# The scan's first loads, clears and diagonal pieces as operations of the stages' plan, in one lasting tile

## The chip, the cores and the metric

The kernel runs on one NeuronCore of a Trainium2 chip. The metric is device time in microseconds, the median of several executions of the same program; lower is better. The profile is one further execution.

## The reference

Eight images of 96 channels and 64 × 64 pixels go through a state-space block with a residual, then through linear attention and a quantized feed-forward, each with a residual. What matters here, cut down:

```python
xi, z = split(layernorm(gn(x)) @ in_proj_w.T + in_proj_b)   # 192 channels each
xi = silu(depthwise_conv3x3(xi) + conv_b)
xs = stack([rows(xi), columns(xi)]); xs = concat([xs, flip(xs)])  # 4 directions, L = 4096
dts, Bs, Cs = split(einsum("bkdl,kcd->bkcl", xs, x_proj_w))       # 6, 16, 16
delta = softplus(dt_proj(dts) + dt_proj_b)
for t in range(L):                                          # 192 channels x 16 states
    h = exp(delta[t] * A) * h + (delta[t] * u[t]) * B[t]
    y[t] = (h * C[t]).sum(states)
out = (layernorm(sum_of_directions(y + D * u)) * silu(z)) @ out_proj_w.T + out_proj_b
```

## The kernel before

The images go in four pairs. For each pair there is a stage and then a scan; a fifth stage finishes the last pair. Between them nothing overlaps but what the queues let through.

**A stage** holds up to five streams of work. For the new pair: `project` (norms, input projection, gate; 16 chunks of 512 positions), `convolve` (3 × 3 depthwise; two channel groups on VectorE in steps at L537 and L540, one on TensorE), `prepare` (states B and C, step sizes delta, delta × u, for 4 directions and 8 chunks in three channel groups, VectorE at L670 to L686; the results `dl`, `du`, `bs`, `cs` go to DRAM). For the old pair: `back` (reads the scan's output `ys` into `yk`, adds directions at L984, norm, gate, output projection, key-value product; 16 units) and `tail` (attention and feed-forward, last add on GpSimd at L1134, store; 16 units). The first stage has no old pair, the last no new one. In the first stage the weights are laid out too, among them the scan's decay matrices `awd`.

**The order in a stage** is made by a planner (`Plan`). Each operation has an engine, an estimated cost, the names that it reads and writes, and a rank. On each engine, among operations that could start within 0.1 us of the earliest by the estimates, that of the lowest rank is put next; so ranks share out an engine, and what is ready fills gaps. The six numbers `FRONT`, `CONV`, `PREP`, `BACK`, `TAIL`, `TAIL_END` set the ranks: project runs from 0 to `FRONT`, convolve from there to `CONV`, prepare from `PREP` to 1, back from 0 to `BACK`, tail from `TAIL` to `TAIL_END`. `P.also` names a gate that every operation added while it is set reads; `gate_off` adds an operation that waits until all of these are done. All DMAs are issued by SP, in the plan's order. A `Slab` cuts one SBUF tile into parts by hand.

**The scan** has an order written out by hand: for 128 steps of 128 positions (4 directions × 32), eight pieces each. A piece is six decay matmuls (`aw` × `dm`, L837), an Exp on ScalarE (L842, L844) and a recurrence on VectorE (L855, 774 columns). GpSimd makes the driving term `dbu` from `dut` and `bc` for two pieces at a time (L819). TensorE then sums the states with a diagonal of C, `cw`: eight of its sixteen column groups are ScalarE copies of `bc` with a mask (L773), eight are small loads (L779), and the rest of those eight is zero from the start (clears at L715, L716). `aw` and `dm` are loaded at L730, L745 and L746, `bc` at L757, `dut` at L792. All these tiles belong to pools that are opened for the scan, in memory that the stage's pools held before; SP issues aw, dm, dut and bc when the stage's last users have let go of it.

Of the kernel before, what the change touches and what calls it, by code (L numbers as in the profile page):

```python
# [19 lines left out]
DIM = 96  # L20
DI = 192
NS = 16
# [16 lines left out]
FRONT = 0.05  # L39
CONV = 0.35  # L40
PREP = 0.08
BACK = 0.7
TAIL = 0.66
TAIL_END = 1.29
NE = 24
X0 = F - 3 * SEG
WC = 256
LOGEXP = "natural_log_exp_and_others"
# [9 lines left out]
class Plan:  # L58
# [9 lines left out]
    def __init__(self):  # L68
        self.ops, self.wrote, self.read = [], {}, {}
        self.free, self.left, self.tiles, self.home = {}, {}, {}, {}  # L70
        self.unit = self.also = None
        self.claims = set()
# [7 lines left out]
    def add(self, engine, cost, emit, reads=(), writes=(), new=(), rank=0.0, kind=None, size=0.0):  # L80
        i = len(self.ops)
        after = set()
        if self.also:
            reads = (*reads, self.also)
# [86 lines left out]
def vss_attn_ffn(ctx: ExitStack, tc: tile.TileContext, a: dict):  # L171
# [96 lines left out]
    class Slab:  # L268


        def __init__(self, pool, name, size):
            self.all, self.at = pool.tile([128, size], F32, name=name), 0
# [46 lines left out]
    def weights(P, wp):  # L319

        P.also = "A3"
# [38 lines left out]
        P.also = None  # L360

    def decay_weights(P, wp):
# [28 lines left out]
        for k in range(KD):  # L391
# [10 lines left out]
            dma(P, 1.6, lambda k=k: awd[k], lambda w=w: P[w].rearrange("p c m n -> p (c m n)"), (w,), (),  # L402
# [16 lines left out]
    def project(P, pair, zs, ybuf, p1, beside):  # L419
# [17 lines left out]
        for b in range(2):  # L437
            mv, gm, gd, gv, gr = stat[b]
            X, S = f"xt{pair}.{b}", f"stat{b}"
            P.also = f"A1.{b}"  # L440
# [67 lines left out]
        P.also = None  # L508
# [4 lines left out]
    def convolve(P, xi, ybuf, p1, beside):  # L513

        P.also = "A2"
# [52 lines left out]
        P.also = None  # L568
# [18 lines left out]
    def prepare(P, tmp, xi, us, dl, du, bs, cs_, beside):  # L587
        P.also = "A2" if beside else "A3"
# [22 lines left out]
        dlv = dl.rearrange("k c a m e t -> k c a (m e) t")  # L611
        duv = du.rearrange("k c m e t -> k c (m e) t")
        for o in range(2):
            for c in range(NCH):
# [14 lines left out]
                for k in (o, o + 2):  # L629
# [17 lines left out]
                    for v, r in ((bs, RK), (cs_, 32 + RK)):  # L647
                        for b in range(2):
                            dma(P, 0.035, lambda v=v, k=k, c=c, b=b: v[
                                    k, 2 * c : 2 * c + 2, NS * b : NS * b + NS].rearrange("j p t -> p j t"),  # L650
                                lambda S=S, r=r, b=b: P[S][64 * b + r : 64 * b + r + NS].rearrange(
                                    "p (j t) -> p j t", j=2), (S,), (), (), rank)
# [12 lines left out]
                    for T in range(3):  # L665
# [7 lines left out]
                        spread(P, 0.26, lambda o, n, k=k, j=j: duv[k, j, o : o + n].rearrange("j p t -> p j t"),  # L673
                               T, lambda q=q: P[q].rearrange("p (j t) -> p j t", t=TC), (q,), (), rank)
# [4 lines left out]
                        def high(name):  # L679
# [11 lines left out]
                        spread(P, 0.39, lambda o, n, k=k, c=c: dlv[  # L691
                                   k, c * F // WC : (c + 1) * F // WC, :, o : o + n
                               ].rearrange("j a p t -> p (j a) t"),
                               T, lambda dp=dp: P[dp].rearrange("p j a t -> p (j a) t"),
                               (dp + "#0", dp + "#1", dp + "#2"), (), rank)


    def scan(dl, du, bs, cs_, ys):
        with ExitStack() as st:
# [6 lines left out]
            quad = st.enter_context(tc.tile_pool(name="s4", bufs=5))  # L706
# [5 lines left out]
            cw = [one.tile([128, 2, NB, 16, TC], F32, name=f"cw{i}") for i in range(2)]  # L712
            for t in da + yp:
                nc.vector.memset(t, 0.0)
            nc.vector.memset(cw[0], 0.0)  # L715
            nc.gpsimd.memset(cw[1], 0.0)  # L716
            da = [t[:, X0 : X0 + W6 + 1] for t in da]

# [5 lines left out]
            aw, dm, bc, dut, dbu, hs, yev = {}, {}, {}, {}, {}, {}, {}  # L724

            def load_aw(k, r):

                aw[k, r] = one.tile([128, NI, 2, 128], BF16, name=f"aw{r}")
                w = 2 * NI * 128
                nc.sync.dma_start(  # L730
                    aw[k, r].rearrange("p i z m -> p (i z m)"), awd[k, :, r * w : r * w + w]
                )

            def load(s, part):
# [4 lines left out]
                if s % 2 == 0 and part == 0:  # L739
                    dm[s // 2] = wk.tile([128, NE, WC], BF16, name="dm")  # L740
                w = NE // 4
                o = 2 * w * (s % 2) + w * part
                v = dl[k, c // 2, :, :, o : o + w].rearrange("a m e t -> (a m) (e t)")
                to = dm[s // 2][:, o : o + w].rearrange("p e t -> p (e t)")
                nc.sync.dma_start(to[0:96], v.unsqueeze(1).to_broadcast([48, 2, w * WC]))  # L745
                nc.sync.dma_start(to[96:128], v[0:32])  # L746

            def load_bc(s):
# [4 lines left out]
                i = s // NB  # L753
                bc[i] = wk.tile([128, 2, 2, NB * TC], F32, name="bc")
                for w, v in ((1, cs_), (0, bs)):
                    for b in range(2):
                        nc.sync.dma_start(  # L757
                            bc[i][64 * b : 64 * b + 64, w].rearrange("p z t -> p (z t)"),
                            v[k, c // NB, 16 * b : 16 * b + 16]
                            .rearrange("(n z) t -> n (z t)", z=2)  # L760
                            .unsqueeze(0).to_broadcast([8, 8, 2 * NB * TC]),
                        )
                        yield

            def diagonal(s):
# [5 lines left out]
                i = s // NB  # L771
                for m in range(8):
                    nc.scalar.activation(  # L773
                        cw[i % 2][:, :, :, m, :].rearrange("p z j t -> p (z j) t"),
                        bc[i][:, 1].rearrange("p z (j t) -> p (z j) t", j=NB),
                        AF.Copy, scale=blk[:, m : m + 1],
                    )
                    m += 8
                    nc.sync.dma_start(  # L779
                        cw[i % 2][8 * m : 8 * m + 8, :, :, m, :].rearrange("p z j t -> p (z j) t"),  # L780
                        cs_[k, c // NB, 16:32].rearrange("(n z) (j t) -> n (z j) t", z=2, j=NB),
                    )
                    yield

            def fetch(g):

                if g >= 4 * N:
                    return
                k, c, _ = steps[g // 4]
                o = NI * (g % 4)  # L790
                dut[g] = quad.tile([128, NI, TC], F32, name="dut")
                nc.sync.dma_start(  # L792
                    dut[g].rearrange("p i t -> p (i t)"),
                    du[k, c, :, o : o + NI].rearrange("m i t -> m (i t)").unsqueeze(1)
                    .to_broadcast([16, 8, NI * TC]),
                )
# [4 lines left out]
            def drive(g):  # L801
# [13 lines left out]
                else:  # L815
# [5 lines left out]
                    dut[g].unsqueeze(1)  # L821
                    .to_broadcast([128, 2, NI, TC]),
                    bc[s // NB][:, 0, :, bass.ts(c % NB, TC)].unsqueeze(2)
# [4 lines left out]
            def decay(p):  # L828
# [7 lines left out]
                for i in range(NI):  # L836
                    nc.tensor.matmul(  # L837
                        e[:, i], aw[k, r][:, i, z, :], dm[s // 2][:, NI * r + i, bass.ts(c % 2, TC)],
# [54 lines left out]
            for r in range(NR):  # L893
                load_aw(0, r)
            for j in range(2):
                load(0, j)
            fetch(0)
            for _ in load_bc(0):
                pass
            fetch(1)  # L900
            for j in range(2):
                load(1, j)
            for _ in diagonal(0):
                pass
            fetch(2)
# [31 lines left out]
    def back(P, pair, ys, us, zs, t1, tn, tmp, psm, kept=None):  # L937
        if kept is None:
            tns = ring(P, tmp, "tns", 3, [DIM + 1, F])
# [8 lines left out]
        yks = ring(P, tmp, "yk", 2, [128, KD, 8, 4 * NE])  # L948
        yds = ring(P, tmp, "yd", 2, [128, 2, 4, 8 * NE])
# [366 lines left out]
```

## Time and profile before

| | us |
|---|---|
| median of 3 runs (10145.36 to 10156.27) | 10145.48 |
| the profiled execution, its own time | 10155.55 |
| its span, first to last instruction | 10153.8 |
| stage 0, to the first recurrence at 529.1 | 529.1 |
| scans (529.1–2310.1, 3028.0–4810.4, 5529.7–7310.5, 8030.1–9807.9) | 1781.0, 1782.4, 1780.8, 1777.8 |
| middle stages between them | 717.9, 719.3, 719.6 |
| last stage | 345.9 |
| busy: VectorE, GpSimd, TensorE, ScalarE | 9133.4, 7542.1, 7238.0, 7028.9 |

A row of the timeline begins with the start and the busy time of a run of like instructions, then engine, line, operation and tiles (out <- in), and in brackets how long the engine was idle before and what ended that. `SPq` is SP issuing a DMA. In the stages many tiles are parts of slabs, so their rows bear the slab's name (`A`), and helpers give one line to many operations (L296 activations, L315 DMAs).

### The profile page before, as it was taken

The numbers are of one execution on the slowest core, as the hardware profiler recorded it, in microseconds if no ns is written. First come the engines' busy times: TensorE is split into PE (matmuls) and PEld (weight loads), VectorE is DVE, ScalarE is ACT, GpSimd is POOL, SyncE is SP. The second block draws the span as 40 slices with busy tenths as digits, with TensorE's granted clock in tenths as the row PEclk, the third lists the DMA queues.
The fourth block names the chain that finished last, engine by engine and source line by source line (L and its number), as shares of the span: only waits on it lengthen the run. The fifth ranks groups of instructions, "written<-read, shape, count | busy, mean of one in ns | idle before, by whom it ended". The sixth has DMA issues, their size and how long they took to land. (4 is left out here: it accounts for less than half of the span.)

```text
span 10153.8 us, 382989 instructions
## 1 busy us (share of the span) xinstructions
PE 7238.0 (71%) x166080; PEld 5184.5 (51%) x166080; DVE 9133.4 (90%) x7072; ACT 7028.9 (69%) x12289; POOL 7542.1 (74%) x2416
## 2 busy tenths in 40 slices
PE   6666676667876667666886666666688666676678
PEld 2155565554425556555442555555543355565554
DVE  7699999997679999999778999999877899999985
ACT  5667777776777777776677777777667777777754
POOL 2099999991039999999104999999810599999971
PEclk7689989998878998988887999998888799988989
DMA  4988888886988888887698888878769788788884
GB/s 132 235 211 215 214 215 213 214 213 138 241 216 213 214 214 216 213 214 188 165 243 211 211 215 213 217 212 214 191 167 240 208 213 216 212 216 214 213 193 102
DMA packets 1593915, 2085.10 MB, mean 205 GB/s; under 512 B 409891, under 2 KB 1050404, under 8 KB 1588644
## 3 DMA queue, kind: packets, MB, share of 16 engines
q1 hardware_dynamic: 1592228, 2060.59, 78.3%
q8 instruction: 1304, 21.36, 1.0%
q14 instruction: 383, 3.14, 0.1%
HBM read 1601.99 MB, written 458.04 MB: 203 GB/s over the span
## 5 line engine op out<-in xcount | busy, mean ns | idle before, releaser
L855 DVE TENSOR_TENSOR_SCAN h<-da,dbu 128x774 f32<-128x774 f32 x4096 | 7025.9, 1759 | 139.5 <-POOL dbu L819 43.5
L819 POOL TENSOR_TENSOR dbu<-dut,bc 128x1536 f32<-128x1536 f32 x2048 | 7083.4, 3575 | 73.6 <-DMA dm<-dl 30.2
L844 ACT ACTIVATE da<-da 128x768 f32<-128x768 f32 x4092 | 3260.2, 797 | 1984.4 <-PE da L837 1968.0
L837 PE MATMUL da<-dm,aw 128*128 128x128 bf16 x24576 | 2279.9, 235 | 2268.3 <-DVE h L855 2078.8
L837 PEld LDWEIGHTS <-aw 128*128 128x128 bf16 x24576 | 1792.8, 104 | 2512.4 <-issue 2233.3
L873 PE MATMUL yp<-h,cw 128*32 128x48 f32 x131072 | 2904.7, 238 | 101.7 <-issue 88.3
L873 PEld LDWEIGHTS yp<-h,cw 128*32 128x32 f32 x131072 | 2412.1, 154 | 548.4 <-issue 228.3
L773 ACT ACTIVATE cw<-bc,blk 128x512 f32<-128x512 f32 x2048 | 1472.4, 720 | 74.3 <-DMA dut<-du 36.0
L984 POOL TENSOR_TENSOR yd<-yk 128x768 f32<-128x768 f32 x64 | 126.7, 1981 | 918.3 <-DMA yk<-ys 630.4
L1134 POOL TENSOR_TENSOR yk<-yk,yd 96x512 f32<-96x512 f32 x64 | 100.1, 1565 | 775.7 <-issue 406.0
L624 POOL COPY A<-A 128x512 f32<-128x512 f32 x96 | 135.7, 1423 | 676.6 <-ACT A L296 375.2
L881 ACT ACTIVATE yev<-yp 128x384 f32<-128x384 f32 x1024 | 505.4, 494 | 81.6 <-PE yp L873 81.3
L296 ACT ACTIVATE A<-A 128x512 bf16<-128x512 bf16 (+1 forms) x777 | 445.8, 618 | 145.1 <-DMA dl<-A 108.6
L816 ACT COPY dbu<-h 128x12 f32<-128x12 f32 x1984 | 409.2, 206 | 0.0
L682 DVE TENSOR_TENSOR A<-A 128x512 f32<-128x512 f32 x384 | 287.2, 751 | 88.6 <-ACT A L296 87.2
L657 PE MATMUL q<-A 6*64 6x512 f32 x1536 | 301.0, 734 | 78.7 <-ACT A L296 65.5
L686 DVE TENSOR_TENSOR A<-A 128x512 bf16<-128x512 f32 x384 | 279.8, 729 | 83.8 <-DMA dl<-A 81.6
L540 DVE SCALAR_TENSOR_TENSOR A<-A,c_convw,A 128x2048 f32<-128x2048 f32 x128 | 299.2, 2363 | 0.6
L998 PEld LDWEIGHTS q<-ident,yd 128*96 128x96 f32 x2048 | 248.1, 169 | 82.9 <-issue 62.2
L998 PE MATMUL q<-ident,yd 128*96 128x128 f32 x2048 | 260.9, 281 | 15.4 <-DVE yd L984 9.3
L296 ACT ACTIVATE A<-q,c_dtb 128x512 f32<-128x512 f32 x384 | 253.7, 677 | 7.0 <-PE q L657 6.0
L411 PE MATMUL q<-small,c_j 96*96 96x512 f32 x384 | 230.1, 693 | 28.8 <-ACT small L296 19.1
(125 smaller groups left out, 5271.8 us busy)
## 6 DMA issues: line engine op xcount, KB each, us to landing
dut<-du SPq DMA_DIRECT2D x2048, 384.0 KB
dm<-dl SPq DMA_DIRECT2D x1024, 288.0 KB
dl<-A SPq DMA_DIRECT2D x256, 384.0 KB
dm<-dl SPq DMA_DIRECT2D x1024, 96.0 KB
ys<-yev SPq DMA_DIRECT2D x1024, 96.0 KB
du<-A SPq DMA_DIRECT2D x256, 256.0 KB
bc<-cs SPq DMA_DIRECT2D x512, 128.0 KB
bc<-bs SPq DMA_DIRECT2D x512, 128.0 KB
```

The costliest lines, as they stand in the source:

```text
L296: "ACT", cost, lambda: nc.scalar.activation(dst(), src_(), func, **kw),
L540: dve(P, 2.34, lambda o=o, v=v, w=w: nc.vector.scalar_tensor_tensor(o, v, w, o, ALU.mult, ALU.add), (), wr, (), first + (CONV - FRONT) / 2 ...
L657: nc.tensor.matmul(P[pqs[T]][o : o + 64], dtw[at : at + RK, k, o : o + 64], P[S][at : at + RK], start=True, stop=True,)
L773: nc.scalar.activation(cw[i % 2][:, :, :, m, :].rearrange("p z j t -> p (z j) t"), bc[i][:, 1].rearrange("p z (j t) -> p (z j) t", j=NB), ...
L816: nc.scalar.copy(start, segs(hs[s - 1][:, :, r])[:, :, :, 1 if back else TC])
L819: nc.gpsimd.tensor_tensor(segs(t)[:, :, :, 1:], dut[g].unsqueeze(1) .to_broadcast([128, 2, NI, TC]), bc[s // NB][:, 0, :, bass.ts(c % NB, ...
L837: nc.tensor.matmul(e[:, i], aw[k, r][:, i, z, :], dm[s // 2][:, NI * r + i, bass.ts(c % 2, TC)], start=True, stop=True,)
L844: nc.scalar.activation(e, e, AF.Exp)
L855: nc.vector.tensor_tensor_scan(hs[s][:, w, r][:, d], da[p % 3][:, o : o + W6][:, d], dbu[4 * s + r][:, w][:, d], 0.0, ALU.mult, ALU.add,)
L873: nc.tensor.matmul(y[32 * q : 32 * q + 32, 2 * NE * i : 2 * NE * i + 2 * NE] .rearrange("p (j r i) -> p i j r", j=2, r=NR), w[:, z, :, t], ...
L881: nc.scalar.activation(yev[s][:, :, o : o + 8, :].rearrange("p j i e -> p i j e"), y[:, 0 : 16 * NE].rearrange("p (i j e) -> p i j e", j=2 ...
L998: nc.tensor.matmul(o, P[yd][:, k, j, DIM * g : DIM * g + DIM], ident, start=(k + j == 0), stop=(k + j == 4),)
```

## The change

One tile `left` now lasts over the whole program. The scan keeps in it `aw`, two `dm`, two `bc`, three of five `dut` and one `cw`; the stages cut their own tiles from the same memory: back's and tail's `yk`, `yd` and one `tns` lie in the part `LT` (under aw, dm and dut 0), back's other tiles and convolve's diagonal in the rest (under bc, dut 1, dut 2 and cw), in the first stage prepare's and the weights' slab from the start of LT into LB, and `small` under cw. Three gates, LT, LB and LC, tell when each part is free. A new function `begin` adds the scan's first loads, one clear and the first eight diagonal pieces to the plan, at rank 2, behind everything else that is ready; the scan no longer issues them. The other `cw` is cleared by half, on VectorE at the scan's start, and of `da` only the boundary columns are. `dl`, `du`, `bs`, `cs` become one DRAM tensor for each direction. The six rank numbers change. Cut to its core:

```diff
-FRONT = 0.05
-CONV = 0.35
-PREP = 0.08
-BACK = 0.7
-TAIL = 0.66
-TAIL_END = 1.29
+FRONT = 0.35
+CONV = 0.54
+PREP = 0.62
+BACK = 0.6
+TAIL = 0.49
+TAIL_END = 1.5
+LT = 4 * 768 + 2 * 3072 + 768
+LB = 2 * 1024 + 2 * 768
...
@@ convolve
-        P.also = "A2"
+        P.also = ("A2", "LB", "LC") if beside else ("A2",)
@@ prepare
-        P.also = "A2" if beside else "A3"
+        P.also = ("A2",) if beside else ("A3", "LB", "LT")
@@ back
+        P.also = ("LB", "LC", "LT")
@@ tail
+        P.also = ("LT",)
...
+    def begin(P, left, dl, du, bs, cs_):
+
+        two, one = Slab(left[:, 0:LT]), Slab(left[:, LT:])
...
+        for name in ("LB", "LC", "LT"):
+            gate_off(P, name)
+        late = 2.0
+        P.add("POOL", 3.5, lambda: nc.gpsimd.memset(cw[:, :, :, 8:16], 0.0), ("LC",), ("cw",), (), late)
+        for at, (to, v) in enumerate(wide_bc(bc[0], bs, cs_, 0, 0)):
+            dma(P, 0.13, lambda to=to: to, lambda v=v: v, ("LB", "bs.0"), (f"bc#{at}",), (), late)
+        for g in (1, 2, 0):
+            to, v = wide_du(dut[g], du, 0, 0, g)
+            dma(P, 0.4, lambda to=to: to, lambda v=v: v, ("LB" if g else "LT", "du.0"), (), (), late)
+        for r in range(NR):
+            to, v = wide_aw(aw, 0, r)
+            dma(P, 0.4, lambda to=to: to, lambda v=v: v, ("LT", "awd0"), (), (), late)
+        for part in range(4):
+            for to, v in wide_dm(dm[0], dl, 0, 0, part):
+                dma(P, 0.2, lambda to=to: to, lambda v=v: v, ("LT", "dl.0"), (), (), late)
+        for m in range(8):
+            (to, v), (to2, v2) = one_block(cw, bc[0], cs_, 0, 0, m)
+            act(P, lambda to=to: to, lambda v=v: v, AF.Copy, 0.72, ("LC", "bc#0", "bc#1", "w_blk"), (f"cw#{m}",), (),
+                late, scale=blk[:, m : m + 1])
+            dma(P, 0.02, lambda to2=to2: to2, lambda v2=v2: v2, ("cw", "bs.0"), (f"cw#{m + 8}",), (), late)
+        return aw, dm, bc, dut, cw
...
-            for t in da + yp:
-                nc.vector.memset(t, 0.0)
-            nc.vector.memset(cw[0], 0.0)
-            nc.gpsimd.memset(cw[1], 0.0)
+            for t in da:
+                nc.vector.memset(t[:, 0 : W6 + 1 : SEG], 0.0)
+            nc.vector.memset(cw[1][:, :, :, 8:16], 0.0)
...
-            for r in range(NR):
-                load_aw(0, r)
-            for j in range(2):
-                load(0, j)
-            fetch(0)
-            for _ in load_bc(0):
-                pass
-            fetch(1)
-            for j in range(2):
-                load(1, j)
-            for _ in diagonal(0):
-                pass
-            fetch(2)
             fetch(3)
             fetch(4)
```

## The prediction

> **What bounds the kernel now.** I read the page first, then busy time by stretch, then the timeline around the hand-over from a stage to the scan, then the waits there.
>
> ```profile
> DVE  7699999997679999999778999999877899999985
> POOL 2099999991039999999104999999810599999971
> ```
>
> These rows of the page's 40 slices show four scans in which VectorE and GpSimd are both full, and five stages between them in which neither is. Inside a scan nothing is to be had: 1756 of 1781 us are VectorE work. The stages and the joints remain. The first middle stage, cut into stretches (columns: stretch, length, busy us of PE, PEld, DVE, ACT and POOL, clock, DMA share, GB/s):
>
> ```profile
> 2327.00:2480.00 153.00, 128.29 (x417) 62.74 (x418) 110.94 (x135) 102.63 (x156) 13.75 (x7) 0.90 0.77 172
> 2480.00:2560.00 80.00, 65.54 (x762) 35.68 (x763) 58.07 (x44) 59.34 (x86) 10.76 (x7) 0.93 0.47 122
> 2560.00:2730.00 170.00, 154.65 (x722) 79.50 (x722) 113.56 (x165) 108.79 (x173) 15.77 (x9) 0.90 0.98 251
> 2730.00:2992.00 262.00, 216.15 (x698) 60.67 (x699) 213.29 (x365) 213.69 (x368) 47.86 (x31) 0.78 0.85 229
> 2992.00:3008.00 16.00, 6.68 (x20) 1.89 (x18) 10.26 (x22) 7.55 (x14) 4.16 (x5) 0.86 0.25 69
> 3008.00:3022.00 14.00, 2.11 (x18) 1.89 (x19) 7.61 (x3) 0.00 (x0) 6.92 (x2) 0.50 0.95 257
> ```
>
> Until 2560 us TensorE is the fullest (84 and 82%) and DMA has room; from 2560 DMA (251, then 229 GB/s) and three engines are all near full. The last two rows are the joint: first DMA idles while the tail's last chains run out, then the engines idle while the scan's first loads run at 257 GB/s. The joint in order of time:
>
> ```profile
> 3004.56 1.15 POOL L1134 TENSOR_TENSOR yk<-yk,yd 96x512 f32<-96x512 f32 x1 [3.44 <-issue]
> ...
> 3007.88 1.78 SPq L730 DMA_DIRECT2D aw<-awd  x4
> ...
> 3010.48 6.88 DVE L715 MEMSET cw<- 128x8192 f32 x1 [1.70 <-issue]
> ...
> 3016.62 2.11 PE L837 MATMUL da<-dm,aw 128*128 128x128 bf16 x18 [13.26 <-DMA dm<-dl]
> ...
> 3022.19 5.00 ACT L773 ACTIVATE cw<-bc,blk 128x512 f32<-128x512 f32 x8 [18.14 <-DMA dm<-dl]
> 3024.27 3.43 POOL L819 TENSOR_TENSOR dbu<-dut,bc 128x1536 f32<-128x1536 f32 x1 [9.35 <-DMA dm<-dl]
> 3027.10 0.79 ACT L842 ACTIVATE da<-da 128x768 f32<-128x768 f32 x1
> ...
> 3037.25 3.43 DVE L855 TENSOR_TENSOR_SCAN h<-da,dbu 128x774 f32<-128x774 f32 x2 [2.47 <-POOL dbu L819]
> ```
>
> The tail's last add ends at 3005.7. SP issues the scan's first load 2.2 us later, when the add's store has landed. The first decay matmul has its weights and steps 8.7 us after that, but its Exp stands on ScalarE behind the eight diagonal pieces, which wait for bc, the late part of the loads; so the first scan starts at 3028.0, 22.3 us after the last work of the stage. The other middle joints repeat it (last adds end 5507.7 and 8007.7, first scans 5529.7 and 8030.1). After stage 0, loads go out at 508.8 and the first scan is at 529.1.
>
> **The change, part by part.** Times are of the profiled execution (span 10153.8, its own time 10155.55 us); the median of the runs is 10145.48, 10 us less, and I apply the differences to the median.
>
> *Diagonal pieces and bc moved up (gate LB/LC: after back and convolve).* The eight ScalarE pieces (5.0 us) and the bc loads leave the path between da and the first scan. In the stage they lie in ScalarE's idle time (492 of 695 us busy); were that cover gone they would cost 5 us. The sixteen-column clear becomes half of one: GpSimd's half, by 6.92/2, 3.5 us in a stage where GpSimd is 14% busy: nothing. VectorE's half, 6.88/2 = 3.4 us, stays at the joint and lies beside the loads.
>
> *Loads that stay behind the tail (gate LT).* dut 0, aw and dm lie where the tail keeps yk, yd and tns, so they wait for its last store as today. Before the first decay SP issued 1920 KB (aw 1536, one pair of dm 384), done 8.7 us after the first issue: 221 KB/us. Now dut 0 goes first: 2304 KB, 10.4 us, so 3018.3; then six matmuls 0.8 and the Exp 0.8 give a first scan at 3020.0. That is 8.0 us earlier. dbu needs dut 0 and bc, there by 3011, and 3.4 us: hidden. The stall of 2.5 us at 3037 (third dut late) goes, since dut 1 and 2 are loaded long before. Together 10.5 us for each middle joint. The Trainium skill's page "DMA: Bandwidth & Descriptors", section "Anatomy of one DMA", prices a transfer at 2.0 us and bytes over 436 GB/s; by it the 2304 KB would be there after 7.4 us, and the joint would gain 13.5 instead of 10.5. The row of 257 GB/s speaks against it.
>
> *What the moved loads cost the stage.* bc, dut 1 and dut 2 (1280 KB) now pass while the steps are stored; at the 229 GB/s of that stretch they take between nothing (share 0.85 leaves room) and 5.7 us. I take 2, nearer to the room. The moved issues, 7 loads and 8 diagonal blocks at 0.6 us (L757, L792), put 9 us into SP's queue, which waited 68 us for ScalarE alone in this stage: nothing. Queued behind each on SP are prepare's stores; a load that stands waiting holds them, and VectorE and ScalarE then wait for their step buffers. The separate DRAM tensors for each direction should leave the loads waiting for direction 0 alone; I price this at nothing, at worst one landing, about 2 us.
>
> *Stage 0.* There prepare itself holds LB and LT, so all loads still follow its last store. Their order is now bc, dut 1, 2, 0, aw, dm: 3584 KB before the first decay instead of 1920. At 205 KB/us (1920 KB took 508.8 to 518.15) that ends at 526.3, at 257 GB/s at 523: first scan at 528 or 525 instead of 529.1, since the diagonal pieces no longer come last. I take 2 us and 2.3 us for the stall 9 us in: 4 us. The last stage has only its memory moved: nothing.
>
> *The ranks.* This is the large unknown. Project's chunks rise from 0 to 0.05 to 0 to 0.33, convolve from 0.05–0.35 to 0.35–0.54, prepare's start from 0.08 to 0.62; back's sixteen units now span 0 to 0.6. So back comes first where project and convolve did. Before, 7 of its units were started by 2560 (7 VectorE adds at L984); by rank, 14 stand ahead of convolve's end. A unit alone costs 12.75 us (16 in 204 us in the last stage); in the stretch 2560 to 2730 it costs 9.2: 170 us less 24 of prepare's step blocks (one direction, chunk and channel group each) at 3.64 (the other 72 in 262 us), over 9 units. Moving x units forward therefore costs 3.5x at most: +25 us for 7. Against it, TensorE idles 39 us before 2560; a unit needs 12.2 us of it (196/16), so 3.2 units could go in free and give back 29 us. I take 0, as the stage's work is the same, and keep −29 to +25 for each of three stages.
>
> Sum: 3 × (−10.5 + 2) − 4 = −30 us: 10115.
>
> **The rivals.** *Hidden altogether.* If the tail now ends before prepare, LT opens early and the loads pass beside the stores. The scan then waits for prepare's memory: its last VectorE op ended at 2987.7; in stage 0 the slab came free 5.4 us after such an op; then the half clear 3.4: first scan at 2996.5, 31 us earlier, and 2.5 for the stall. The 4.6 MB of loads cost up to 20 us of DMA at 229 GB/s, say 10. 3 × −24 − 4 gives 10070. For it: tail ranks now begin at 0.49, against: they end at 1.5, after all of prepare.
>
> *Back ahead of convolve.* Place: TensorE from 2327 to 2560. Prepare cannot start before project and convolve end, and its stores are what fills DMA from there on. With 7 units ahead the stage is 25 us longer: +75 − 30, 10190. The joints' gain is used up at 2.9 units (10 us a stage); over 0.2% slower from 4.8. For it: the new ranks say so, and DMA has room only early. Against: the early stretches are no better filled today, and a list that takes whatever is ready fills gaps.
>
> *Loads behind the tail again.* The change does not do what it says: 3.4 MB of 4.6 stay behind LT, and tail ranks up to 1.5 let the tail end some 8 us later, so the wait only changes its name: −30 + 24, about 10140.
>
> **How the numbers follow.** About 0.2%, 20 us, can be told from no change. Forecast (10115) 0.36; hidden 0.16; loads behind the tail 0.15; back ahead of convolve 0.33. Faster 0.52, same 0.15, slower 0.33. The forecast's own range is 10085 to 10125. The range goes down to 10015, hidden with nearly two thirds of the best packing of 3 × 29 (10070 − 55), and up to 10195, the slow case with 5 us over.
>
> **What would show it.** Right: the first scan 10 us nearer to the tail's last add; no ScalarE piece L773 in the joint; bc and the clear inside the stage; the stall after the fourth scan gone. The stage's length from the scan's end to its last add (695.6 us before) decides among the rivals: over 712, back was ahead. Wrong altogether: a slower scan (over 1785 us), or SP waits on the new loads while prepare's stores stand behind.

## The result, and the profile after

The changed kernel takes 10073.33 us (median of 6 runs, 10064.43 to 10080.79), the kernel before 10147.75 beside it (6 runs). The ratio is 0.9928, 95% interval 0.9918 to 0.9938: 74 us less, where 30 were forecast. The profiled execution has a span of 10072.0 us.

The page's rows that answer to the two shown of before look much the same:

```profile
DVE  6689999997789999999778999999977899999985
POOL 2089999993129999999114999999801599999971
```

The four scans are as full and as long as they were, 1781.5, 1783.0, 1780.7 and 1775.3 us. The difference lies between them. Busy time by stretch of the first middle stage and its joint (columns as before: stretch, length, busy us of PE, PEld, DVE, ACT and POOL, clock, DMA share, GB/s):

```profile
2343.00:2500.00 157.00, 142.36 (x591) 79.56 (x592) 112.94 (x147) 97.88 (x149) 20.03 (x10) 0.95 1.02 218
2500.00:2626.00 126.00, 114.79 (x945) 61.57 (x944) 107.29 (x101) 96.07 (x146) 16.04 (x8) 0.97 0.57 140
2626.00:2730.00 104.00, 92.87 (x439) 40.93 (x437) 72.51 (x112) 72.69 (x122) 10.75 (x6) 0.89 0.86 239
2730.00:2977.00 247.00, 201.91 (x632) 50.81 (x630) 199.69 (x341) 209.58 (x358) 55.17 (x33) 0.76 0.88 236
2977.00:2994.00 17.00, 3.49 (x8) 0.70 (x6) 13.81 (x29) 14.55 (x24) 1.48 (x1) 0.50 0.98 263
2994.00:3012.00 18.00, 1.97 (x18) 1.78 (x19) 4.34 (x3) 2.22 (x4) 7.85 (x6) 0.50 1.00 287
```

TensorE is 91% busy until 2626 us, where it was 84 and 82% before. And the stretch in which DMA idled at 69 GB/s, while the tail ran out alone, is no longer there: the last 35 us of stage and joint move 263 and 287 GB/s at a share of 0.98 to 1.00. The joint in order of time:

```profile
2992.23 1.48 POOL L1165 TENSOR_TENSOR left<-left 96x512 f32<-96x512 f32 x1 [22.87 <-issue]
...
2994.24 0.69 DVE L688 TENSOR_TENSOR A<-A 128x512 bf16<-128x512 f32 x1 [1.46 <-DMA dl<-A]
...
2997.04 1.57 SPq L316 DMA_DIRECT2D dl<-A  x2
2998.66 0.96 SPq L316 DMA_DIRECT2D left<-du  x1
2999.72 2.23 SPq L316 DMA_DIRECT2D left<-awd  x4
...
3002.00 6.79 SPq L316 DMA_DIRECT2D left<-dl  x8
3002.52 3.47 DVE L788 MEMSET cw<- 128x4096 f32 x1 [7.59 <-issue]
3004.11 3.43 POOL L859 TENSOR_TENSOR dbu<-left 128x1536 f32<-128x1536 f32 x1 [2.36 <-DMA left<-du]
...
3010.03 2.23 PE L877 MATMUL da<-left 128*128 128x128 bf16 x18 [19.27 <-DMA left<-dl]
3010.93 0.80 ACT L882 ACTIVATE da<-da 128x768 f32<-128x768 f32 x1 [15.56 <-issue]
...
3011.82 1.77 DVE L895 TENSOR_TENSOR_SCAN h<-da,dbu 128x774 f32<-128x774 f32 x1 [5.83 <-ACT da L882]
```

Tail (L1165, ended 2993.7) and prepare (L688, ended 2994.9) now end together. The loads behind LT follow prepare's last store, the decay matmul waits for the first `dm` among them (`left<-dl`), its Exp has no diagonal piece ahead of it, and the first recurrence starts 16.9 us after the last work, where it was 22.3.

All kernels in one table. A stage's length runs from a scan's end to the next first recurrence; the column "prepare, tail" has the starts of prepare's last step (its first VectorE operation, L670 in before; the step's last one starts 2 to 4 us later) and of tail's last add, after the scan's end, in the first middle stage; the joint is the time from the stage's last VectorE or GpSimd operation to the first recurrence, in that stage.

| kernel | median | ratio to before, 95% | stage 0 | middle stages | prepare, tail | joint |
|---|---|---|---|---|---|---|
| before | 10147.75 | | 529.1 | 717.9 719.2 719.7 | 674, 694 | 22.3 |
| after | 10073.33 | 0.9928 (0.9918–0.9938) | 544.8 | 685.5 688.5 693.8 | 664, 666 | 16.9 |
| before_newranks | 10071.53 | 0.9929 (0.9914–0.9944) | 535.5 | 698.8 692.6 692.9 | 669, 658 | 25.2 |
| after_oldranks | 10223.96 | 1.0079 (1.0062–1.0095) | 586.5 | 724.2 725.5 727.3 | 665, 710 | 13.3 |
| after_loads_in_scan | 10130.16 | 0.9989 (0.9979–0.9998) | 541.5 | 705.1 707.7 704.8 | 676, 646 | 24.7 |
| after_one_dram | 10073.96 | 0.9931 (0.9916–0.9946) | 539.8 | 689.1 689.6 691.1 | 667, 669 | 18.2 |
| after_split | 10068.54 | 0.9936 (0.9921–0.9951) | 541.7 | 688.7 687.4 694.7 | 666, 667 | 19.1 |
| after_split_oldranks | 10176.18 | 1.0037 (1.0023–1.0051) | 538.8 | 728.1 727.4 729.2 | 668, 714 | 12.9 |
| before_front | 10115.81 | 0.9978 (0.9968–0.9987) | 534.7 | 709.0 709.5 712.2 | 680, 622 | 24.4 |
| before_back | 10232.14 | 1.0095 (1.0080–1.0110) | 530.3 | 755.1 756.7 743.0 | 725, 698 | 25.0 |
| after_names | 10151.82 | 1.0007 (0.9998–1.0017) | 555.6 | 714.0 714.9 712.5 | 700, 668 | 9.7 |
| after_order | 10151.00 | 1.0006 (0.9997–1.0016) | 539.6 | 718.0 714.3 716.9 | 704, 671 | 9.3 |
| after_tailend | 10162.29 | 1.0022 (1.0012–1.0032) | 540.3 | 719.3 718.7 718.1 | 704, 617 | 10.1 |
| after_fixed_order | 10103.86 | 0.9964 (0.9951–0.9978) | 535.4 | 700.9 699.1 697.8 | 674, 663 | 23.0 |

The kernel before was run beside each group; its medians there lie between 10136.96 and 10142.11, and each ratio is to its own. One caution for all of it: the scans of kernels whose scan code is the same add up to 7122.0 us in the profile of before and to 7103.4 in that of before_front, so sums over profiles say nothing below some 20 us.

### The profile page after: what moved, and what is told of

Same layout as the page of the kernel before. It is cut to its first block, busy times and chain, and to the rows that moved or that the text cites. A ratio compares the mean times of both kernels' runs of the same rounds, so it can differ in the third digit from the quotient of the medians.

```text
span 10072.0 us, 383210 instructions
## 1 busy us (share of the span) xinstructions
PE 7220.6 (72%) x166080; PEld 5173.8 (51%) x166080; DVE 9099.3 (90%) x7064; ACT 7011.9 (70%) x12277; POOL 7554.2 (75%) x2416
## 5 line engine op out<-in xcount | busy, mean ns | idle before, releaser
L859 POOL TENSOR_TENSOR dbu<-left 128x1536 f32<-128x1536 f32 x1232 | 4312.6, 3581 | 90.4 <-DMA left<-du 61.6
L877 PE MATMUL da<-left 128*128 128x128 bf16 x24576 | 2290.4, 236 | 2256.6 <-DVE h L895 2055.0
L877 PEld LDWEIGHTS <-left 128*128 128x128 bf16 x24576 | 1796.8, 104 | 2501.9 <-issue 2213.2
L859 POOL TENSOR_TENSOR dbu<-dut,left 128x1536 f32<-128x1536 f32 x816 | 2873.0, 3581 | 13.9 <-ACT dbu L856 7.9
L913 PE MATMUL yp<-h,left 128*32 128x48 f32 x65536 | 1460.2, 238 | 47.8 <-issue 47.5
L913 PE MATMUL yp<-h,cw 128*32 128x48 f32 x65536 | 1452.0, 239 | 37.9 <-issue 24.6
L913 PEld LDWEIGHTS yp<-h,left 128*32 128x32 f32 x65536 | 1209.6, 153 | 276.3 <-issue 123.8
L913 PEld LDWEIGHTS yp<-h,cw 128*32 128x32 f32 x65536 | 1207.7, 154 | 262.7 <-issue 97.9
L827 ACT ACTIVATE cw<-left,blk 128x512 f32<-128x512 f32 x1024 | 738.5, 721 | 0.0
L827 ACT ACTIVATE left<-left,blk 128x512 f32<-128x512 f32 x992 | 715.9, 722 | 0.0
L1165 POOL TENSOR_TENSOR left<-left 96x512 f32<-96x512 f32 x64 | 99.8, 1559 | 586.4 <-DVE left L1163 417.9
```

The costliest lines, as they stand in the source:

```text
L827: nc.scalar.activation(to, v, AF.Copy, scale=blk[:, m : m + 1])
L859: nc.gpsimd.tensor_tensor(segs(t)[:, :, :, 1:], duts[g % 5].unsqueeze(1) .to_broadcast([128, 2, NI, TC]), bcs[s // NB % 2][:, 0, :, bass.t ...
L877: nc.tensor.matmul(e[:, i], aw[r][:, i, z, :], dms[s // 2 % 2][:, NI * r + i, bass.ts(c % 2, TC)], start=True, stop=True,)
L913: nc.tensor.matmul(y[32 * q : 32 * q + 32, 2 * NE * i : 2 * NE * i + 2 * NE] .rearrange("p (j r i) -> p i j r", j=2, r=NR), w[:, z, :, t], ...
```

## The experiments

### Which part of the change gained

Four kernels, each with one part of the change alone or undone. **before_newranks**: the kernel before with the six numbers of after.

```diff
-FRONT, CONV, PREP, BACK, TAIL, TAIL_END = 0.05, 0.35, 0.08, 0.7, 0.66, 1.29
+FRONT, CONV, PREP, BACK, TAIL, TAIL_END = 0.35, 0.54, 0.62, 0.6, 0.49, 1.5
```

> The kernel before with the six new rank numbers and nothing else. Theory R (the ranks made both the 28 us that each middle stage lost and the 17 us that the first stage gained; moved loads gave some 4 us a joint, the lasting tile 7 us in the last stage): first recurrence at about 545 instead of 529 us, middle stages (scan's end to first recurrence) 688 to 696 instead of 719, last stage 346 as before; time about 10148 + 16 - 3 x 26 = 10086. Theory L (the moved loads and what they free made the middle stages shorter, the ranks little): middle stages 715 to 722, time 10145 to 10165.

**after_oldranks**: the reverse, the changed kernel with the old numbers.

> The changed kernel with the six old rank numbers. Theory R: first recurrence back at 526 to 529 us, middle stages 707 to 715 (only the joints shorter, 4 to 11 us), last stage 339; time about 10148 - 2 - 3 x 8 - 7 = 10115. Theory L: middle stages stay at 685 to 694, time about 10055 to 10073.

**after_loads_in_scan**: the changed kernel, but the loads, the clear and the diagonal pieces are issued by the scan again, in the order of before.

```diff
@@ begin
-        P.add("POOL", 3.5, lambda: nc.gpsimd.memset(cw[:, :, :, 8:16], 0.0), ...
-        for at, (to, v) in enumerate(wide_bc(...)): dma(...)
...
@@ scan
+            nc.gpsimd.memset(cw[0][:, :, :, 8:16], 0.0)
+            for r in range(NR):
+                load_aw(0, r)
...
```

> The changed kernel (its memory, gates, DRAM tensors and ranks), but the plan holds none of the scan's loads, clears and diagonal pieces: the scan issues them itself in the old order, GpSimd clears its half of cw there. Theory R: from the stage's last add to the first recurrence some 22 us instead of 18, middle stages 689 to 696, time 10085 to 10095, that is 4 to 8 us for each of three middle joints. Theory L: middle stages back to 712 or more, time over 10140.

**after_one_dram**: the changed kernel with `dl`, `du`, `bs` and `cs` as one DRAM tensor each.

```diff
-new[name] = [dram.tile(shape, dtype, name=f"{name}{k}") for k in range(KD)]
+whole = dram.tile([KD, *shape], dtype, name=name)
+new[name] = [whole[k] for k in range(KD)]
```

> The changed kernel with dl, du, bs and cs as one DRAM tensor for all four directions again. If the separate tensors matter (a moved load of direction 0 then waits for the latest store of any direction, and prepare's stores queue behind it on SP): a gap in SP's issues near 2730 to 2750 us, middle stages 3 to 15 us longer, time 10080 to 10120. If they don't: 10073 within 0.1%, same order and same waits.

The six numbers alone give the whole effect: 10071.53, as fast as the changed kernel. Without them the rest of the change makes the kernel slower, 10223.96, which neither theory had foreseen. One DRAM tensor or four makes no difference. after_loads_in_scan lies between, 57 us above after: so the layout looked costly and the move looked like a repair of it. That reading is not shown: without the moved operations the planner also puts the others in another order (in the first middle stage VectorE's part at the 368th of 724, clears not counted).

The rest of the change is not idle either; its parts cancel. Against before_newranks, the profile of after has middle stages that are 5.5 us shorter on average (689.3 against 694.8), joints of 17 us instead of 25, but a stage 0 that is 9.3 us longer; the 12 us by which its scans are longer (7120.5 against 7108.5) are within what equal code differs by. In after_oldranks, where the tail still ends last as it did before, the joints are 13.3, 13.7 and 12.3 us, some 9 less than before; but the tail's last add comes 15 us later after the scan's end (710 against 694), and the stage is longer all the same. What makes the tail late there was not found.

Where do the six numbers gain? Three stretches of the first middle stage of before, and the same three of before_newranks:

```profile
2370.00:2430.00 60.00, 52.48 (x183) 26.01 (x181) 31.90 (x41) 48.65 (x71) 6.03 (x3) 0.97 0.72 164
2430.00:2490.00 60.00, 51.16 (x138) 22.98 (x138) 52.97 (x49) 42.03 (x65) 2.19 (x1) 0.89 0.41 109
2490.00:2550.00 60.00, 46.68 (x681) 27.36 (x680) 50.26 (x34) 40.98 (x60) 7.18 (x4) 0.91 0.45 104
```

```profile
2374.00:2434.00 60.00, 58.46 (x252) 33.69 (x251) 34.12 (x48) 44.14 (x65) 9.23 (x5) 1.00 1.14 249
2434.00:2494.00 60.00, 57.37 (x254) 32.67 (x252) 55.26 (x56) 38.23 (x58) 7.89 (x4) 1.00 0.70 163
2494.00:2554.00 60.00, 59.23 (x363) 30.57 (x364) 45.29 (x53) 48.67 (x75) 4.67 (x3) 1.00 0.66 168
```

VectorE and ScalarE do the same work in both (135 and 131 us of 180); TensorE does 175.1 us instead of 150.3, and DMA 193 GB/s on average instead of 126. Those are back's units, put into holes that project and convolve leave: 240 us after the scan's end 12 of the 16 adds that back has on VectorE have started, 7 in before. What it frees is time at the end: prepare's last operation comes 4 us earlier in this stage, and the tail, which ended 18 us after it (3005.7 against 2987.7), now ends before it. The granted clock is 1.00 in the rows where TensorE is 97% busy and 0.89 to 0.97 in those where it is 83%. The Trainium skill's page "TensorE: Matmul & The Clock Gate", Part 1, says that activity of the array releases its throttle; these rows agree.

### Which of the six numbers

**before_front** has FRONT, CONV and PREP of after, **before_back** BACK, TAIL and TAIL_END.

> The kernel before with FRONT 0.35, CONV 0.54 and PREP 0.62 of after, but BACK, TAIL and TAIL_END of before. Theory M (the new ranks gain because back's units are done before prepare starts: a unit costs 9.3 us there and 12 in prepare's mix, so what counts is PREP behind most of BACK): 14 of 16 units lie ahead of PREP, so nearly the whole gain of the six numbers: 10075 to 10090, middle stages 692 to 700. Rival T (the gain is the tail's, started earlier and ended with prepare): middle stages stay at 715 or more, 10140. Stage 0, which knows only these three numbers, is at 535 instead of 529 by both.

> The kernel before with BACK 0.6, TAIL 0.49 and TAIL_END 1.5 of after, but FRONT, CONV and PREP of before. Theory M: prepare still starts at 0.08 among back's units, so little changes: 10130 to 10145, middle stages 712 to 718. Rival T: middle stages 692 to 700, 10070 to 10085. Stage 0 at 529 by both.

Both theories fell. Three numbers alone are worth 21 us, the other three alone cost 95, and together they gain 69: neither half is the mechanism. The starts of the last operations say why. In before_front TensorE is filled early as well (170 us of the same 180), but the tail's last add comes 58 us before prepare's last step, and what prepare leaves unused at its end nobody fills: DMA moves 203 and 195 GB/s in two late stretches of 60 us (first two rows), against 215 and 232 in those of before_newranks (next two). In before_back the ranks of back run from 0 to 0.6 and prepare's start at 0.08, in between; one early stretch (last row) runs at 68 GB/s with every engine at 80% or less, and prepare ends 51 us later than in before.

```profile
2849.00:2909.00 60.00, 49.38 (x158) 13.18 (x155) 50.35 (x91) 49.90 (x87) 15.88 (x11) 0.89 0.75 203
2909.00:2969.00 60.00, 45.16 (x152) 9.82 (x149) 47.50 (x73) 42.06 (x75) 25.47 (x13) 0.69 0.74 195
...
2854.00:2914.00 60.00, 50.49 (x155) 12.57 (x157) 52.09 (x81) 47.21 (x83) 23.79 (x13) 0.72 0.80 215
2914.00:2974.00 60.00, 47.54 (x150) 10.68 (x146) 50.47 (x83) 48.20 (x85) 19.50 (x9) 0.59 0.89 232
...
2486.00:2546.00 60.00, 47.79 (x654) 27.43 (x652) 39.48 (x30) 32.43 (x49) 7.46 (x2) 0.81 0.27 68
```

In these four kernels the stage is short where the early stretch is full and prepare and tail end close together, and that took both halves. It is a reading that fits the four; no run changed one of the two conditions alone.

### The one tile

In after_oldranks stage 0, where there is no back and no tail, is 57 us longer than before. Its waits between 30 and 200 us (columns: engine, tile and line, what was waited for, us in total, times, longest) have three rows, the last three here, that before has not:

```profile
DVE A L416 <- ACT left L297: 59.1, 7, 22.8
...
ACT left L297 <- DMA left<-ad: 42.8, 5, 24.0
...
PE q L412 <- DMA left<-ad: 31.2, 2, 27.1
DVE A L416 <- DMA left<-ad: 29.7, 2, 20.2
```

Project's `small` lies in `left`, under LC; the weights' transfers (`ad`) go to another part of `left`. Nothing of the one is read by the other, and yet project waits for them. **after_split** cuts `left` into three tiles, **after_split_oldranks** does so with the old numbers.

```diff
-    left = lead.tile([128, LT + LB + 8192], F32, name="left")
+    left = [lead.tile([128, n], F32, name=f"left{i}") for i, n in enumerate((LT, LB, 8192))]
```

> The changed kernel with `left` cut into three tiles (the parts under LT, LB and LC) instead of one; ranks, moved loads and gates as after. Theory F (the one shared tile makes operations of one part wait for transfers into another: project's `small` in stage 0 waits for the weights' DMAs, back and tail for one another's): stage 0 ends at 535 instead of 545, the middle stages, 685 to 694 long, lose some 8 us each, the four scans, 7120 together, come back to 7109; 10 + 24 + 11 less than 10073: about 10028, and surely under 10055. Rival N (the cost lies in the order that the planner makes of the added gates and names, not in the memory): within 10 us of 10073, stage 0 still at 540 or more.

> As the kernel with three tiles, but with the six rank numbers of before. With one tile this was 10224, stage 0 586 long and the middle stages 724 to 727. Theory F: stage 0 comes back to 530 to 535 (the waits of up to 30 us for the weights go) and the middle stages to 712 or less: 10224 - 53 - 40 = about 10130. Rival N: within 15 us of 10224, stage 0 over 575.

With the old numbers stage 0 comes back from 586.5 to 538.8 and the time falls by 48 us: the waits through the shared tile are real, and that is their price. The order cannot be the cause: in both traces every engine's operations, and SP's transfers, follow in the same order in stage 0 and in the first middle stage. TensorE's busy time in those 170 us rises from 93.97 to 120.32 (after_oldranks, then after_split_oldranks):

```profile
30.00:200.00 170.00, 93.97 (x143) 31.02 (x141) 75.79 (x65) 70.57 (x105) 43.24 (x4) 0.66 0.25 83
...
30.00:200.00 170.00, 120.32 (x733) 46.09 (x731) 118.77 (x89) 96.80 (x145) 46.75 (x5) 0.77 0.31 102
```

With the new numbers the split brings nothing that can be told (10068.54), and the middle stages do not move in either pair: there the theory is wrong.

### The moved loads, and the order

**after_names** changes only the names by which the planner knows prepare's first stores. In after all stores of a kind write one name, so the planner takes them to follow one another.

```diff
-    ("du.0",) if k + c == 0 else ()
+    P.first("du", k + c == 0)          # du.0.0, du.0.1, ...; the loads read them all
```

> The kernel with `left` in three tiles (10068.5), and one thing more: each transfer of direction 0's first chunk writes a name of its own in the plan (bs.0.0, bs.0.1, ...), and the scan's first loads read them all, where all of a kind wrote the one name bs.0, du.0 or dl.0. Theory C (writers of one name are put one after another by the planner, 2 us a transfer by its estimates, so prepare's first steps are put late: in stage 0 its 9th step starts at 230 instead of 225 and its 17th at 247 instead of 241, and the 8 us are never made up): stage 0 541.7 - 8 = 534; the middle stages, 687 to 695, win between nothing and 5 us each; 10045 to 10060. Rival N (the order differs by chance, wherever a gate or a name is added): stage 0 stays over 538 and the time within 8 us of 10068.

**after_order** has the loads in the order of use as well, **after_tailend** instead TAIL_END 1.4.

> As after_names, and the scan's first loads in the order of their use: bc, then for each of the four weight blocks its dut, its aw and its two dm loads, instead of three dut, all aw, all dm. Theory J (the first scan waits for bytes ahead of the first dm part): in the middle joints 1152 KB instead of 2304 lie ahead of the first decay, at 257 to 287 KB/us 4 us less each; in stage 0 1664 KB instead of 3584, 7 us less; 7 + 12 less than after_names. Rival K (the bytes are only wanted later: the scan stalls at its 3rd, 5th and 7th recurrence for the blocks behind): the first recurrence comes as early, but the stalls take half or more of it back, 0 to 9 us less than after_names.

> As after_names with TAIL_END 1.4 instead of 1.5: tail ends earlier, so the part LT comes free before prepare's last step. Theory H (the rival `hidden altogether` of the prediction: then dut 0, aw and dm pass beside prepare's stores and the joint is only prepare's end, the clear and the first decay): tail's last add 10 us or more before prepare's last step, joint 9 to 12 us instead of 18, prepare 2 to 4 us later for the traffic: 9 to 15 us less than after_names in the three joints. Rival D (transfers are near full in that stretch, share 0.88 to 0.98 at 236 to 263 GB/s, so the loads push prepare's stores back by as much as they come forward): within 6 us of after_names, prepare's end 5 us or more later.

The theory of after_names failed by its whole size and in its sign: 83 us slower than after_split, for no operation more. In stage 0 prepare's 17th step (its first VectorE operation) starts at 285.0 us, 12.6 us later than in after_split and not earlier. The two halves of a store for the third channel group still wrote one name, so the chain was thinned and not removed; what it did was to change the order (in the first middle stage VectorE's operations part from those of after_split at the 301st of 724). This is what makes after_loads_in_scan, after and after_names hard to compare: each has another order of a stage's operations, and an order, the loads' places in it included, can be worth 80 us.

For the joint the three runs are instructive. Here the tail ends 32, 33 and 87 us before prepare's last step; LT comes free early, as in the rival that was called hidden altogether, and joints of 16.9 us become 9 to 10. The stage pays. SP's issues in after_names:

```profile
3017.12 0.56 SPq L330 DMA_DIRECT2D dl<-A  x1
3017.77 0.56 SPq L330 DMA_DIRECT2D du<-A  x1
3018.38 1.15 SPq L330 DMA_DIRECT2D left<-du  x1
3019.63 2.21 SPq L330 DMA_DIRECT2D left<-awd  x4
...
3022.86 1.31 SPq L330 DMA_DIRECT2D dl<-A  x2
3024.28 0.73 SPq L330 DMA_DIRECT2D du<-A  x1
3025.22 4.77 SPq L330 DMA_DIRECT2D left<-dl  x5
3030.11 0.38 SPq L330 DMA_DIRECT2D dl<-A  x1
```

The stores (`dl<-A`, `du<-A`) stand between and behind the loads into `left`. Busy time by stretch of that end, and the waits in it:

```profile
3005.00:3041.00 36.00, 8.20 (x46) 2.98 (x42) 18.24 (x31) 19.18 (x33) 4.12 (x1) 0.50 0.99 286
```

```profile
ACT A L311 <- DMA dl<-A: 16.6, 7, 8.2
DVE A L702 <- DMA dl<-A: 15.5, 7, 7.4
```

With DMA at 0.99 VectorE does 18.2 us of work in 36 and waits 15.5 us for its step buffers to be stored. In after_split the stretch up to prepare's end had no LT loads in it and took 18 us for 14.3:

```profile
2975.00:2993.00 18.00, 3.42 (x6) 0.71 (x6) 14.30 (x30) 15.52 (x26) 1.48 (x1) 0.50 0.99 266
```

That is 18 us more for 3.9 us more of work, while the joint is 9.4 us shorter. As far as two kernels of different order can be compared, the loads cost the stage at least what they save the joint. In stage 0, where they cannot pass early, after_order shows the order of use alone: the joint is 16.8 us against 22.3 in after_names, 5.5 of the 7 expected, but 2.6 us of them come back as gaps between the recurrences of the scan's first 60 us (4.0 us against 1.4), as rival K said. The whole kernel is no faster than after_names (10151.00 and 10151.82), where theory J had 19 us less. The tail's earlier end in after_tailend won nothing more: joints of 10.1, prepare's end 4 us later, and 10162.29, 10 us slower, where theory H had 9 to 15 less.

**after_fixed_order** then holds the order. The moved operations get engines of their own in the planner, without cost, and no two stores share a name; on every engine the other operations stand in the order of before_newranks.

```diff
+    def behind(P, size, out_, in_, ...):
+        P.add("begin SP", 0.45, lambda: nc.sync.dma_start(out_(), in_()), ..., size=-size)
...
-        P.add("POOL", 3.5, ...
+        P.add("begin POOL", 3.5, ...
-            act(P, ...
+            P.add("begin ACT", 0.72, ...
```

> The change's structure with the order held: the scan's first loads, clear and diagonal pieces are put among the stages' operations, in the order of their use as in after_order and with `left` in three tiles, but the planner gives them engines of their own without cost, and no two of prepare's transfers write one name; so on every engine the other operations stand in exactly the order of before_newranks (10071.5). Theory P (the moved loads are worth what the prediction's steps say, and the 80 us between after_split and after_names are the order's, not theirs): prepare's last operation 2 to 5 us later than in before_newranks (2987, 5462, 7928 from the start of the program, counted from each scan's end), joints of 10 us instead of 23.5 to 25.2 in the middle and 17 instead of 25.8 in stage 0: 3 x (14.5 - 3.5) + 9 = 42 us less, about 10030, within 10015 to 10045. Rival Q (the transfers of that stretch are the bound, so that 4.6 MB of loads push prepare's stores back by as much as the joint wins): prepare's end 12 us or more later, 10060 to 10075. Rival R (the loads themselves disturb the stage, whatever the order): middle stages over 705 us as in after_names, 10110 or more.

10103.86: 32 us slower than before_newranks, whose order it has, and no theory's number. In the profiles, 26 us apart, the middle stages are 4.5 us longer on average and the scans 16 us longer in sum, which is within what equal code differs by. In the middle stages prepare's last operation comes 4.2, 8.0 and 8.7 us later, between theory P's 2 to 5 and rival Q's 12, and the joints hardly shrink (23.0, 22.0 and 21.2 us instead of 23.5 to 25.2). In stage 0 the two cancel: the joint is 7.8 us shorter and prepare's end 7.6 us later. For the middle joints the timeline has the reason:

```profile
3000.70 0.69 DVE L711 TENSOR_TENSOR A<-A 128x512 bf16<-128x512 f32 x1 [1.24 <-DMA dl<-A]
...
3007.33 0.80 ACT L904 ACTIVATE da<-da 128x768 f32<-128x768 f32 x1 [5.50 <-PE da L899]
...
3012.91 2.43 SPq L332 DMA_DIRECT2D dl<-A  x3
...
3020.34 0.12 POOL L876 MEMSET dbu<- 128x12 f32 x1 [31.50 <-DMA dl<-A]
3020.54 3.43 POOL L881 TENSOR_TENSOR dbu<-left,left 128x1536 f32<-128x1536 f32 x1
...
3024.45 6.69 DVE L917 TENSOR_TENSOR_SCAN h<-da,dbu 128x774 f32<-128x774 f32 x4
```

The first decay is ready at 3008, 16 us before the recurrence that needs it. But `dbu` lies in memory that prepare held, and prepare's last three stores are issued 11 us after the work that made them, because thirteen loads stood among prepare's last stores on SP, nine of them issued after that work was done. The gap between the last work and the first decay closed; a gap between the last store and the first `dbu` opened. In after the loads came behind the last store; the same wait ended at 3001.6 there, and `dbu` starts at 3004.1. From 2997 to 3013 us SP itself waited 4.3 us for earlier transfers to land, and the rest went into issues. The Trainium skill's page "DMA: Bandwidth & Descriptors", section "Anatomy of one DMA", says that a transfer's wait is made on the issuing sequencer before dispatch; that fits SP's rows here, where stores whose data is ready are late by the issues and waits of the loads ahead.

## Why the prediction was right and wrong, step by step

The sign was right, and the time lies inside the range. The sum was not: −30 was made of joints, and −74 is what the ranks make alone. That the two have one sign is luck.

- **The ranks, taken at 0, are the mis-sized term.** They measure 24 us a middle stage (718.9 to 694.8 on average), close to the bound of −29. The step's row was the right one, TensorE idle before 2560 us, and its argument for 0, that the stage's work is the same, was the error: 24.7 us of that idle time were filled (175.1 less 150.3). The other bound, +25, rested on a unit costing more early than in the mix with prepare; five more units went early, and prepare still ended 4 us sooner. In the first middle stage the sum is plain: 18.0 us of the tail's run-out and 4.0 of prepare went, the joint grew by 2.9, and the stage is 19.1 us shorter.
- **The joint is right in kind.** Its first recurrence was to come 8.0 us nearer to the last work, 14.3 instead of 22.3; it came to 16.9, 17.1 and 17.7. From the first LT load to the first recurrence it is 13.2 us where 12.1 were worked out. What was missing is that these loads now queue behind prepare's last stores: the first goes out 3.7 us after the last work, where it was 2.2 us in the kernel before. Where the tail ends last, as the step assumed, the joints are 12.3 to 13.7 us (after_oldranks), 1 to 2 under the step's 14.3. No ScalarE piece is left in the joint, as said. The fit that the prediction took from the Trainium skill's page "DMA: Bandwidth & Descriptors", section "Anatomy of one DMA", and that gave 7.4 us for these bytes, is stated there for transfers issued from GpSimd. Here SP issues them, and 11.4 us pass from the first issue to the first decay matmul.
- **The moved loads' cost of 2 us** is neither shown nor refuted. The last work of the middle stages comes 672.1 us after the scan's end in after and 670.2 in before_newranks, which agrees, but the three stages of after lie between 668.6 and 676.0, and the two kernels have different orders. No run moves bc, dut 1 and dut 2 alone. For LT's loads among prepare's stores the runs show no room.
- **The stall at 3037 us**, after the scan's fourth recurrence, is gone: from 3011.8 us at least 15 recurrences follow one another in one row of the timeline. But its 2.5 us a scan do not show: the scans sum to 7120.5 us, 7122.0 before.
- **Stage 0**, put at −4, became +15.7: 6.4 from the ranks (535.5), 3.1 from the shared tile (541.7 when split), and the other 6.2, it seems, from the order: with the order held and the tile split it is 535.4. The step had not asked what the new numbers do where there is no back.
- **The last stage**, put at nothing, is 7.0 us shorter (338.9), 4.8 of them with the ranks alone. The cause was not looked for.
- **The separate DRAM tensors** at nothing: right, 10073.96 without them.
- **Rivals.** Back did go ahead of convolve, and the stage from scan's end to the tail's last add fell from 695.6 to 667.4, so that rival's price is refuted. Hidden altogether had the right number, 10070, by luck: in after the LT loads pass behind all stores, and where the rival's condition came true (joints of 9 to 10 us) the kernel was slower.

What stays open is why after_names' order makes prepare slower before any LT load passes. In the 283 us from 2667 VectorE does 206.6 us of work, in after_split from 2653 in as many 224.7; more of its waits are for `dl` stores (31.5 us against 10.7 over the whole stretch), but which swap of operations begins it was not found. Whether a better order exists for the moved loads, with LT's loads behind the last store and the order of use, was not tried; no version here is measurably faster than after and before_newranks, so no run shows a gain in time from the moved loads.

## What to carry to other kernels

Where a planner puts out the order, read its order as part of the change: names, gates and added operations move everything else, and only a run with the order held tells the change from its shuffle. A wait at a joint that is filled with transfers may only move with them: here joints of 9 to 10 us went with a slower stage, while the transfers passed where DMA was full. Whether moving them pays where DMA idles, no run here isolates. Their place in the issuing queue counts too: with the loads among the last stores, the stores were late. Filling the engine that idles early, with the two streams that close a stage ending close together, went with 69 us less here, for six numbers.

## What the runs showed that was not expected

Project's operations waited up to 27.1 us for transfers into another part of the same tile, and three tiles instead of one took 48 us off the kernel with the old numbers. In after, prepare's last stores and the loads of the joint ran at 263 and 287 GB/s with the DMA share at 0.98 to 1.00, above the 257 (0.95) of the joint before. The clear of half a `cw` took 3.47 us on VectorE, half of the 6.88 of a whole one, as worked out.
